# Two convolution layers on one core: every engine in the order of issue, stores a step behind, loads placed by hand

## The chip, the cores and the metric

The kernel runs on one core of a Trainium2 chip. A core has TensorE (PE, matrix multiply, with its weight loads shown as PEld), VectorE (DVE), ScalarE (ACT), GpSimd (POOL) and SyncE (SP). SP issues all of this kernel's data transfers; they run on 16 DMA engines. The metric is the device time of one execution in microseconds (us), as a median of runs. The profile is of one further execution.

## The reference

The input x is 4 x 512 x 64 x 64 in float32. Layer 0 is a linear attention with a convolved second set of heads; layer 1 takes edge maps of the result, mixes channels and normalizes.

```python
# layer 0
qkv = concat(h @ wq.T, h @ wk.T, h @ wv.T)             # channels last, then moved back
dw  = conv(qkv, dw_kernel, 5x5, groups=1536)
pw  = conv(dw, pw_kernel, 1x1, groups=192)
f   = concat(qkv, pw).reshape(B, -1, 24, N)            # 128 heads of 8
query, key, value = relu(f[:, :, :8]), relu(f[:, :, 8:16]), f[:, :, 16:]
scores = einsum('bhdn,bhen->bhde', pad_ones(value), key)
out = einsum('bhde,bhen->bhdn', scores, query)
out = out[:, :, :-1] / (out[:, :, -1:] + 1e-15)
y = batchnorm(conv(out, proj_kernel, 1x1)) + x
# layer 1, on y
sobel = sqrt(sobel_h**2 + sobel_v**2 + 1e-8); lap = abs(dwconv(y, K_LAP))
diag = max(abs(dwconv(y, K_D1)), abs(dwconv(y, K_D2)))
grad = sqrt(sobel**2 + lap**2 + 1e-8)
ef = gelu(bn(einsum('kbchw,koc->kbohw', stack(sobel, lap, diag, grad), w_branch)))
att = sigmoid(gelu(ef.mean((2, 3)) @ w_att1.T + b_att1) @ w_att2.T + b_att2)
z = einsum('bchw,oc->bohw', ef * att, w_fuse) + b_fuse
out = gelu(layernorm_over_channels(z) * ln_gamma + ln_beta) + y
```

## The kernel before

**Tiling.** Each of the 4 batches has 4 groups of 128 channels of q, k and v. An image is cut into 8 strips j of 512 positions (two halves of 4 strips; strip k of a half holds every fourth row). A 128x512 tile in float32 is the usual unit; a matrix product of that size is two passes of PE.

**The front: layer 0.** For each of the 16 groups `keys_and_values` and then `queries` list steps. In `keys_and_values` the steps are `project(KEY, j)` and `values(j)` for each strip, with transposes (`turn`) and `scores` behind them, and between these the second half of the previous group's convolution work (the list entries made by `q`). `project` (L250) multiplies a strip of x by the group's weights; ACT copies the result to `strip`, and four transfers put it into `inp`, the padded image that `convolve` reads. `values` (L273) ends in four stores to `near`, a DRAM image of the values' neighbourhoods. `convolve` (L382) is the 5x5 convolution as 160 small products in two passes, 320 matmuls and as many weight loads a call; each group has a call for KEY, half 0 and 1, in `queries`, and for QUERY, half 0 and 1, in the following `keys_and_values`. `correlate` (L432) multiplies turned keys by a `near` buffer of 1 MB; two calls use one buffer, and `load_near` (L420) fetches buffers in order into three slots. `denominators`, `invert` (an add and a reciprocal, L353 and L354), `spread_out` (the `over` matmuls) and `divide` make the quotient; `fold` and `conv_fold` make the output projection's weights, stored in `folded`. `mix` (L469) loads `projc` and multiplies it for batch 0.

**The stages behind: the rest.** For a finished batch three generators follow: `project_out` (Y, L599: sums eight `hd` tiles with `fold_sb` to y, adds x from `xr`, stores it from `yt`), `edge_branches` (E, L654: for each window of four rows two calls of `edges`, one for each half of the channels, and two of `branches`) and `fuse_out` (F, L746: attention, the last product, layer norm, output). Each `yield` gives the worth of a step; `advance` (L868) takes steps from the head of the list `behind` as the front earns due time, at a rate `pace`. What a batch has left when the front ends is done in a tail: 16 steps of the last batch's Y, then its E with one step of whatever remains (Y, then the F of batch 2) after each of its steps, then its own F.

**What sets the order.** PE runs in the order in which the program issues its instructions:

```python
    ctx.enter_context(tc.manual_schedule(engines={mybir.EngineType.PE}))
```

The order on ACT, DVE, POOL and on SP's queue is chosen at compile time by a scheduler that moves an instruction ahead of others when it expects it to be ready. On each engine, once so ordered, an instruction that waits holds all those behind it. A tile's buffer is free when its last reader is done; a load into it waits for that.

Of the kernel before, what the change touches and what calls it, by code (L numbers as in the profile page):

```python
# [65 lines left out]

WAIT_Y, WAIT_E, WAIT_F = 20.0, 12.0, 16.0
# [13 lines left out]
def conv_seq_kernel(  # L81
# [16 lines left out]
    ctx.enter_context(tc.manual_schedule(engines={mybir.EngineType.PE}))  # L98
# [72 lines left out]

    def load_constants():
        nc.sync.dma_start(out=consts_sb, in_=consts)
        nc.sync.dma_start(out=vec_sb, in_=vec)
        nc.sync.dma_start(out=batt1_sb, in_=batt1)

        nc.scalar.activation(inv0, vec_sb[:, V_BNV, :], AF.Sqrt, bias=bn0_eps)
        nc.vector.reciprocal(inv0, inv0)
# [3 lines left out]

        gamma_row = work_tile("gamma_row")
        nc.sync.dma_start(out=inv0_row, in_=bn0[1])
        nc.sync.dma_start(out=gamma_row, in_=bn0[0])
        nc.scalar.activation(inv0_row, inv0_row, AF.Sqrt, bias=bn0_eps)
# [25 lines left out]

    xs = {}

    class Group:
# [15 lines left out]
        def load_mat(self, t):  # L231

            dp = gw.tile([P, 4, 48], F32, name="dp_sb", tag="dp_sb", bufs=2)
            nc.sync.dma_start(out=dp, in_=dpk[self.g, t // QUERY])
            self.mat[t] = gw.tile([P, 4, 40, 8], F32, name="mat", tag="mat")
# [7 lines left out]
        def load_x(self, j):  # L243
            xs[self.b, j] = []
            for n in range(2):
                xt = xst.tile([P, 2, 512], F32, name="xt")
                nc.sync.dma_start(out=xt, in_=x[self.b, j, :, 2 * n : 2 * n + 2, :])
                xs[self.b, j] += [xt[:, 0, :], xt[:, 1, :]]

        def project(self, t, j):  # L250
            half, k = STRIPS[j]
            if (self.b, j) not in xs:
                self.load_x(j)
# [5 lines left out]
            if t == QUERY and not (j in KV_ORDER[:2] and self.g < NG - 1):  # L259
                del xs[self.b, j]  # L260
# [4 lines left out]
            for n in range(4):  # L265
                nc.sync.dma_start(out=inps[t][r::4, n, b : b + 8, :], in_=rows(s)[32 * n : 32 * n + 32, :, :])
# [6 lines left out]
        def values(self, j):  # L273
# [8 lines left out]
            if j not in Q_ORDER[:2]:  # L282
                del xs[self.b, j]
# [5 lines left out]
            for a in range(2):  # L289
                for jp in range(2):  # L290
                    nc.sync.dma_start(
                        out=self.near_dram[jp, b + a : b + a + 7 : 2, 2 : W + 2, (k + 2) % 4, :].rearrange(
                            "c x d -> x c d"
                        ),
                        in_=vt[64 * a : 64 * a + 64, :, 2 * jp : 2 * jp + 2, :].rearrange("p c q d -> p c (q d)"),
                    )
# [36 lines left out]
        def fold_turn(self):  # L333
# [4 lines left out]
            nc.scalar.copy(self.st, t_ps[:, 0:P])  # L338
            self.p = work_tile("p")
            nc.sync.dma_start(out=self.p, in_=proj[self.g])  # L340

        def fold(self):
# [4 lines left out]
            nc.sync.dma_start(out=self.folded[0, :, self.g, :], in_=f)  # L347
# [24 lines left out]
        def divide(self, half):  # L372
            banks = self.spread_out(self.rec)
            for k in range(4):
# [3 lines left out]
                nc.sync.dma_start(out=self.heads[j, :, self.g, :], in_=q)  # L378
# [53 lines left out]
        def correlate(self, half, jp, step):  # L432
# [17 lines left out]
            if step % 2:  # L450
                del self.near[half, jp, b]
                self.load_near(1)
# [16 lines left out]
        def mix(self):  # L469

            self.pc = work_tile("pc")
            if self.b:
                nc.sync.dma_start(out=self.pc, in_=mixed[self.g])
                return
            rest = work_tile("projc")
            nc.sync.dma_start(out=rest, in_=projc[self.g])
            pw = mini.tile([P, 8], F32, name="pw")
            nc.sync.dma_start(out=pw, in_=pwk[self.g])
            pwb = mini.tile([P, 16, 8], F32, name="pwb", bufs=1)
            nc.vector.tensor_mul(  # L480
                pwb, bdmask.rearrange("p (h d) -> p h d", d=8), pw.unsqueeze(1).to_broadcast([P, 16, 8])
            )
            ps = ps_tile("mix")
            nc.tensor.matmul(ps, lhsT=pwb.rearrange("p h d -> p (h d)"), rhs=rest, start=True, stop=True)
            nc.scalar.copy(self.pc, ps)
            nc.sync.dma_start(out=mixed[self.g], in_=self.pc)
# [32 lines left out]
        def conv_fold(self):  # L519
# [5 lines left out]
            nc.sync.dma_start(out=self.folded[1, :, self.g, :], in_=f)  # L525
# [502 lines left out]
```

## Time and profile before

| | us |
|---|---|
| median of 3 runs | 5160.07 (5154.5 to 5172.19) |
| the profiled execution | 5156.95 |
| its span, first to last instruction | 5155.2 |
| SP, time spent in issuing transfers | 1953 |

| engine | busy us | share of the span |
|---|---|---|
| PE | 4721.2 | 92% |
| PEld (overlaps PE) | 2727.4 | 53% |
| DVE | 2125.2 | 41% |
| ACT | 1622.7 | 31% |
| POOL | 384.0 | 7% |

An engine's busy time doesn't count its waits. A row of waits names the engine and line that stood idle, what ended the wait, the total, the number of times and the longest. "issue" means that the wait ended with nothing that the profile shows. A row of a timeline gives start, duration, engine, line, operation and tiles, and in brackets the idle time before it. TensorE's clock is given as a share of full speed. 910 MB went over the DMA engines in the span, 177 GB/s on average.

### The profile page before, as it was taken

The page shows a single profiled execution, that of the slowest core. Times are in us where ns is not written, and L with a number is a line of the kernel's source. Part 1 is how long each engine was busy: PE and PEld are TensorE (multiplying, and loading weights), DVE is VectorE, ACT ScalarE, POOL GpSimd, SP SyncE. Part 2 cuts the span into 40 slices and gives each one's busy share as a digit, 9 for nine tenths or more (in the row PEclk, how much of TensorE's full clock was granted, in tenths as well). Part 3 has the DMA queues.
Part 4 walks back from the last instruction along what each step waited for, and adds up shares of the span by engine and source line. Part 5 has one row for each costly group of instructions (what it writes and reads, how often), then busy time and mean ns, then how long its engine had stood idle before and what let it go on. Part 6 is the DMA issues. An engine that isn't in the chain of part 4 may idle for free. (4 is left out here: it accounts for less than half of the span.)

```text
span 5155.2 us, 107053 instructions
## 1 busy us (share of the span) xinstructions
PE 4721.2 (92%) x46362; PEld 2727.4 (53%) x46362; DVE 2125.2 (41%) x2960; ACT 1622.7 (31%) x2585; POOL 384.0 (7%) x291
## 2 busy tenths in 40 slices
PE   7899999998999999799999998989989998899877
PEld 4556555454566655344466655444446565345443
DVE  1222221113655625211456543431135556246975
ACT  1111111001444524200235442430024445125765
POOL 0000000000000003200000000320000000000225
PEclk9999999999999999899999999999999999899989
DMA  6777777775666666767667666567666665674535
GB/s 184 187 193 195 185 212 191 179 160 140 194 184 193 194 191 188 212 153 150 168 178 208 170 191 186 180 202 172 154 177 173 178 183 160 176 179 117 153 103 169
DMA packets 645992, 910.30 MB, mean 177 GB/s; under 512 B 323688, under 2 KB 394376, under 8 KB 627088
## 3 DMA queue, kind: packets, MB, share of 16 engines
q1 hardware_dynamic: 645520, 903.45, 65.5%
q8 instruction: 364, 5.96, 0.5%
q14 instruction: 108, 0.88, 0.1%
HBM read 622.13 MB, written 213.98 MB: 162 GB/s over the span
## 5 line engine op out<-in xcount | busy, mean ns | idle before, releaser
L256 PE MATMUL proj<-xt,w_sb 128*128 128x512 f32 x2048 | 959.6, 611 | 58.3 <-DMA xt<-in_x 47.2
L642 PE MATMUL yps<-hd,fold_sb 128*128 128x512 f32 x2048 | 904.3, 598 | 25.2 <-DMA hd<-heads 23.1
L390 PE MATMUL cv<-inp,mat 32*32 32x512 f32 x20480 | 771.7, 621 | 121.2 <-issue 112.0
L256 PEld LDWEIGHTS proj<-xt,w_sb 128*128 128x128 f32 x2048 | 382.8, 195 | 534.8 <-issue 457.1
L642 PEld LDWEIGHTS yps<-hd,fold_sb 128*128 128x128 f32 x2048 | 385.8, 191 | 510.5 <-issue 474.2
L390 PEld LDWEIGHTS cv<-inp,mat 32*32 32x32 f32 x20480 | 422.1, 105 | 433.5 <-issue 270.8
L717 PE MATMUL br<-maps,wbr_sb 128*128 128x256 f32 x2048 | 491.6, 393 | 56.6 <-ACT maps L700 33.7
L278 PEld LDWEIGHTS val<-w_sb,xt 128*128 128x128 f32 x4096 | 471.5, 192 | 31.6 <-issue 21.9
L717 PEld LDWEIGHTS br<-maps,wbr_sb 128*128 128x128 f32 x2048 | 395.6, 196 | 173.5 <-issue 55.8
L278 PE MATMUL val<-w_sb,xt 128*128 128x128 f32 x4096 | 484.1, 276 | 0.1
L795 PE MATMUL zps<-ef,wf_sb 128*128 128x512 f32 x1024 | 462.6, 604 | 21.0 <-DVE z L799 7.2
L262 ACT COPY strip<-proj 128x512 f32<-128x512 f32 x256 | 149.3, 583 | 1017.1 <-PE proj L256 952.8
L647 DVE SCALAR_TENSOR_TENSOR yt<-yps,shift,xr 128x512 f32<-128x512 f32 x128 | 96.1, 751 | 905.1 <-PE yps L642 833.7
L442 PE MATMUL corr<-near,ckt 128*32 128x160 f32 x8192 | 330.7, 313 | 28.1 <-DMA near<-near 23.0
L236 POOL TENSOR_TENSOR mat<-dp_sb 128x1280 f32<-128x1280 f32 x32 | 77.3, 2416 | 3484.1 <-PE cv L390 2959.3
L795 PEld LDWEIGHTS zps<-ef,wf_sb 128*128 128x128 f32 x1024 | 194.2, 193 | 263.8 <-issue 227.8
L442 PEld LDWEIGHTS corr<-near,ckt 128*32 128x32 f32 x8192 | 252.4, 110 | 130.0 <-issue 58.2
L690 DVE TENSOR_TENSOR maps<-dv 128x1054 f32<-128x1054 f32 x128 | 162.6, 1270 | 304.1 <-PE br L717 304.1
L724 ACT ACTIVATE ef_o<-br,shift,scale 128x256 f32<-128x256 f32 x256 | 142.4, 560 | 314.9 <-PE br L717 314.4
L306 ACT ACTIVATE kt<-tr 128x512 f32<-128x512 f32 x128 | 76.1, 595 | 496.5 <-PE tr L304 488.9
L354 DVE RECIPROCAL rec<-rec 128x512 f32<-128x512 f32 x64 | 214.5, 3351 | 1.4
L402 ACT ACTIVATE co<-cv 128x512 f32<-128x512 f32 x128 | 74.6, 597 | 438.5 <-PE cv L390 438.4
(124 smaller groups left out, 4096.6 us busy)
## 6 DMA issues: line engine op xcount, KB each, us to landing
xt<-in_x SPq DMA_DIRECT2D x400, 512.0 KB
near<-near SPq DMA_DIRECT2D x128, 1056.0 KB
inp<-strip SPq DMA_DIRECT2D x1024, 64.0 KB
win<-y SPq DMA_DIRECT2D x128, 396.0 KB
near<-vt SPq DMA_DIRECT2D x512, 66.0 KB
y<-yt SPq DMA_DIRECT2D x128, 264.0 KB
yr<-y SPq DMA_DIRECT2D x128, 264.0 KB
xr<-in_x SPq DMA_DIRECT2D x128, 256.0 KB
```

The source lines that it names most:

```text
L256: nc.tensor.matmul(ps, lhsT=self.w[t][:, c, :], rhs=xs[self.b, j][c], start=(c == 0), stop=(c == NCH - 1))
L262: nc.scalar.copy(s, ps)
L278: nc.tensor.matmul(ps[:, ts(c, P)], lhsT=xs[self.b, j][n][:, ts(c, P)], rhs=self.w[VALUE][:, n, :], start=(n == 0), stop=(n == NCH - 1),)
L354: nc.vector.reciprocal(rec, rec)
L390: nc.tensor.matmul(rows(banks[i])[32 * j : 32 * j + 32, :, c0:c1], lhsT=self.mat[t][q, j, (dx + 2) * 8 + 4 * b : (dx + 2) * 8 + 4 * b + 4, :],
L442: nc.tensor.matmul(self.banks[jj][32 * i : 32 * i + 32, 160 * b : 160 * b + 160], lhsT=self.held["c", i][:, at : at + 32], rhs=v[:, 4 * n ...
L642: nc.tensor.matmul(ps, lhsT=fold_sb[g // NG][:, g % NG, ts(c, P)], rhs=hd[g], start=(g == 0), stop=(g == 2 * NG - 1),)
L647: nc.vector.scalar_tensor_tensor(yt[:, :, 1 : W + 1], rows(ps), shift0[:, c : c + 1], rows(xr), ALU.add, ALU.add)
L690: nc.vector.tensor_sub(flat[:, half : 3 * half - 2], dvs[:, 2 : 2 * half], dvs[:, 0 : 2 * half - 2])
L717: nc.tensor.matmul(rows(ps)[:, 4 * n : 4 * n + 4, :], lhsT=wbr_sb[:, k, c, :], rhs=rows(maps[c // 2][:, slot[k], c % 2, :], WB)[:, :, 0:W] ...
L724: nc.scalar.activation(o[:, n, :], ps[:, 256 * n : 256 * n + 256], AF.Gelu, bias=shift1[:, k : k + 1], scale=scale1[:, k : k + 1], accum_o ...
L795: nc.tensor.matmul(ps, lhsT=wf_sb[:, k, ts(c, P)], rhs=ef[k], start=(k == 0), stop=(k == 3))
```

## The change

The whole program becomes manual: all engines and SP run in the order of issue. A list `waiting` holds closures with a step number; `later` appends, `tick`, called after every step, issues those whose step has come. `send` is a store put off in this way by a step, and all stores but the zero borders go through it.

- Loads of x follow a fixed list `x_order`, half a strip each. Five are issued at the start; `done_x` asks for two more a step after a strip's last use. Before, `project` loaded a strip that wasn't there.
- `load_near`, `load_w`, `load_mat`, `load_p`, `load_pc` and `load_wtab` become entries of worth 0 in the lists of steps; `correlate` no longer loads. `make_mat` on POOL comes three steps after its load. The constants' arithmetic comes three steps after their loads, the zero borders of `near` at steps 6 and 14.
- Y loads `fold_sb` in eight pieces, each followed by an `hd` tile, a step each; `xr` is loaded one step ahead, with 2 buffers for 3; `yt` has 3 buffers for 2.
- E is cut by half windows p (channel half and four rows) into `load_window`, `columns`, `across`, `laplacian`, `gradient` and `roots`; the gradient and roots of p-1 come with the `across` of p, the branches of a window a step later still. The operations are the same. With the last batch a flush of all waiting stores stands before each window load.
- F loads `ef` with 7 buffers for 8 (three tiles of the next strip after the first product, the rest after the last). `norm` becomes `variance`, a reciprocal a step later and `finish` for one or two channel tiles at a time, over two strips' steps; `z` has 8 buffers for 6, `sq` 2 for 3.
- The tail issues 22 steps of the F of batch 2 beside the first 24 of Y (8 of them its loads), and then spreads the rest over E in proportion to `FILL_Y` and `FILL_F`.

```diff
+FILL_Y, FILL_F = 1.5, 3.5
+REST = 16 * FILL_Y + 11 * FILL_F
...
-    ctx.enter_context(tc.manual_schedule(engines={mybir.EngineType.PE}))
+    ctx.enter_context(tc.manual_schedule())
+    waiting, clock = [], [0]
+    def later(issue, steps=1):
+        waiting.append((clock[0] + steps, issue))
+    def tick(whole=False):
+        clock[0] += 1
+        ready = [w for w in waiting if whole or w[0] <= clock[0]]
+        waiting[:] = [w for w in waiting if not (whole or w[0] <= clock[0])]
+        for _, issue in ready:
+            issue()
+        if whole and waiting:
+            tick(True)
+    def send(out, in_, steps=1):
+        later(lambda: nc.sync.dma_start(out=out, in_=in_), steps)
...
+    def done_x(b, j):
+        del xs[b, j]
+        later(lambda: load_x(2))
...
             if step % 2:
                 del self.near[half, jp, b]
-                self.load_near(1)
...
         def queries(self):
...
-                pj(0), own("scores", KV_ORDER[6]), own("turn", KV_ORDER[7]), pj(1), cv(0), pj(2), own("scores", KV_ORDER[7]), ct(0, 0), ct(0, 1), pj(3),
-                ct(0, 2), ct(0, 3), own("denominators", 1), own("fold_turn"), pj(4), own("divide", 1), pj(5), co(0, 0),
-                own("fold"), pj(6), co(0, 2), co(1, 0), co(1, 2), cv(1), pj(7), ct(1, 0), ct(1, 1), own("denominators", 0),
-                ct(1, 2), ct(1, 3),
+                pj(0), own("scores", KV_ORDER[6]), own("turn", KV_ORDER[7]), ld("load_mat", QUERY), pj(1), cv(0), pj(2),
+                ld("load_w", KEY, of=after), own("scores", KV_ORDER[7]), ct(0, 0), ct(0, 1), pj(3), near, ct(0, 2), ct(0, 3),
+                own("denominators", 1), ld("load_p"), own("fold_turn"), near, pj(4), own("divide", 1), near,
+                ld("load_w", VALUE, of=after), pj(5), co(0, 0), near, co(0, 2), own("fold"), pj(6), co(1, 0), co(1, 2), cv(1),
+                pj(7), ct(1, 0), ct(1, 1), near, own("denominators", 0), ct(1, 2), ct(1, 3),
...
         def keys_and_values(self, before):
...
+                pj(KEY, 0), near(before), q("conv_sums"), ld("load_mat", KEY), pj(VALUE, 0), near(before), q("divide", 0),
+                ld("load_w", QUERY), pj(KEY, 1), pj(VALUE, 1), co(0, 0), tr(0), near(before), pj(KEY, 2), co(0, 2),
+                pj(VALUE, 2), sc(0), tr(1), co(1, 0), pj(KEY, 3), co(1, 2), ld("load_wtab"), ld("load_pc", of=before),
...
     def project_out(b, heads, cheads, folded, side):
...
+            for g in range(2 * NG):
+                nc.sync.dma_start(out=fold_sb[g // NG][:, g % NG, :], in_=folded[g // NG, :, g % NG, :])
+                load(0, g + 1)
+                yield WAIT_Y / (2 * NG)
...
     def edge_branches(b, efs, pool_sb, side):
...
+            load_window(0)
+            yield WAIT_E
+            for p in range(4 * NJ + 2):
+                ready = p // 2 - 1 if p >= 2 and p % 2 == 0 else None
+                if p < 4 * NJ:
+                    columns(p)
+                    load_window(p + 1)
+                    yield 3.0 * share
+                if 1 <= p <= 4 * NJ:
+                    gradient(p - 1)
+                if p < 4 * NJ:
+                    across(p)
+                if 1 <= p <= 4 * NJ:
+                    roots(p - 1)
+                    yield 4.5 * share
+                if ready is not None:
+                    branches(ready, (1, 2))
+                    yield 1.5 * share
+                if p < 4 * NJ:
+                    laplacian(p)
+                    yield 5.0 * share
+                if ready is not None:
+                    branches(ready, (0, 3))
+                    del maps[2 * ready], maps[2 * ready + 1]
+                    yield 1.5 * share
+            tick(True)
...
     next(fused)
     next(edged)
-    for _ in range(1 + NCH * NJ // 2):
-        next(projected)
-    rest = [projected] + behind
-    for n, _ in enumerate(edged):
-        while rest and next(rest[0], None) is None:
-            rest.pop(0)
+    for n in range(6 + NCH * NJ // 2):
+        next(behind[0])
+        tick()
+        for _ in range(1 if n >= 6 else 2 if n >= 2 else 0):
+            next(projected)
+            tick()
+    rest, spent, given = [projected] + behind, 0.0, 0.0
+    for share in edged:
+        tick()
+        given += share * REST / SHARE_E
+        while rest and spent < given:
+            step = next(rest[0], None)
+            if step is None:
+                rest.pop(0)
+            else:
+                spent += FILL_Y if rest[0] is projected else FILL_F
+                tick()
```

## The prediction

> **What bounds the kernel now.** I read the page first, then TensorE's waits, then the places that the long waits point to.
>
> ```profile
> span 5155.2 us, 107053 instructions
> PE 4721.2 (92%) x46362; PEld 2727.4 (53%) x46362; DVE 2125.2 (41%) x2960; ACT 1622.7 (31%) x2585; POOL 384.0 (7%) x291
> core 0: 5155.2 us, clock 0.963
> ```
>
> TensorE (PE) is the bound: busy for 4721 us, idle for 434. The second loss is in the clock. A window that isn't at 1.00 is at 0.50, so a mean of 0.963 is 0.037 x 2 x 5155 = 381 us at half rate, of which PE was busy for about 251 by the trace's clock records: some 126 us of slowness on top of the idle time. The change leaves the arithmetic as it is, so all that it can win is in these 434 + 126 = 560 us. TensorE's waits by what ended them:
>
> ```profile
> PE cv L390 <- issue: 112.0, 46, 4.4
> PE proj L256 <- DMA xt<-in_x: 47.2, 14, 12.1
> PE br L717 <- ACT maps L700: 33.7, 9, 10.2
> PE over L369 <- DVE rec L354: 23.6, 16, 4.6
> PE yps L642 <- DMA hd<-heads: 23.1, 6, 9.8
> PE corr L442 <- DMA near<-near: 23.0, 7, 19.6
> PE heads_ps L511 <- ACT strip L262: 20.4, 1, 20.4
> PE mix L484 <- DMA projc<-in_projc: 14.2, 4, 4.9
> ```
>
> The first row counts most: in `convolve` PE waited 112 us for nothing that the profile names. I cut the convolve matmuls into their 64 calls. The second KEY half takes 19.0 us on average, the first KEY half 11.4, the two QUERY halves 12.3 and 13.0, an undisturbed call 10.6. Of the 121 us of such idle time inside the calls, 78 lie in that one call of each group. Windows over an undisturbed call (first row) and three of the slow ones; columns are window, length, busy time of PE, PEld, DVE, ACT and POOL, clock, share of the DMA engines, GB/s:
>
> ```profile
> 679.00:689.60 10.60, 10.60 (x321) 6.54 (x320) 0.00 (x0) 1.09 (x2) 0.00 (x0) 1.00 0.70 226
> 161.00:181.00 20.00, 13.70 (x321) 6.81 (x317) 1.82 (x4) 0.59 (x2) 0.00 (x0) 0.91 0.84 210
> 352.00:369.00 17.00, 13.22 (x324) 7.35 (x321) 2.10 (x4) 0.39 (x1) 0.16 (x1) 0.90 0.98 247
> 2600.00:2618.00 18.00, 14.75 (x324) 7.82 (x320) 2.06 (x4) 0.00 (x0) 0.00 (x0) 0.81 0.83 194
> ```
>
> The timeline of SyncE (SP), then of PE, around the last of these says why:
>
> ```profile
> 2590.23 0.57 SPq L427 DMA_DIRECT2D near<-near  x1
> ...
> 2594.02 1.22 SPq L427 DMA_DIRECT2D near<-near  x2
> ...
> 2600.19 0.52 SPq L427 DMA_DIRECT2D near<-near  x1
> ...
> 2600.05 7.13 PE L390 MATMUL cv<-inp,mat 32*32 32x512 f32 x182
> 2610.44 7.92 PE L390 MATMUL cv<-inp,mat 32*32 32x504 f32 x138 [3.25 <-issue]
> ```
>
> Four `near` loads of 1 MB are issued in the 10 us up to this call's start. A convolve call issues 640 instructions in 10.6 us[...]. The page's queue list has an instruction queue, q8, with 364 packets of 16 KB[...]. In the trace a q8 packet starts about 2.6 us before most of these waits end, and the DMA engines were nearly full for the 6 us before it. I read the row as instruction blocks stuck behind bulk loads.
>
> **The change part by part.** A minus is time saved.
>
> (A) `near` loads. Before, every second `correlate` fetches the next buffer, so three or four of these megabytes land just before or in `convolve(KEY, 1)`. After, three are issued from `project(3)` to `divide`, the fourth after the first `correlate` pair, the fifth only after that call and the last projection. The call should come down to a QUERY call's 12.5: 16 x (19.0 - 12.5) = -104. The fourth now flows under the second correlate pair, which is as dense (128 instructions in 2.45 us): a third of a 3.3 us stall each, +19. Sum -85. Ends: 0 if density alone makes the stall, -134 if the call reaches 10.6. [...]
>
> (B) `mix`: projc is loaded right where it is used; after, `load_pc` issues it some five steps and one 10.6 us call ahead. -14.2, and half a 3.4 us half-rate window after each of four: -6.8. Sum -20.
>
> (C) Start: at 26.5 us PE waits 12.1 for the second strip of x, since SP stood at a store of `vt` with the x loads behind it. After, two and a half strips are issued first. -13 with the clock.
>
> (D) heads_ps, 20.4 at 1247: ACT held four relus of a convolve that ended at 1217 behind three half-windows of edge work. In order of issue the relus come first. With the clock -22.
>
> (E) `near` at 2165, 19.6: the load waited on SP behind eight `hd` and two `fold_sb` transfers. After, the four-step lead covers most; the 16 transfers still share the engines. -15.
>
> (F) x loads elsewhere: 47.2 - 5.6 (first load, stays) - 12.1 (C) = 29.5. After, a load follows the release of its buffer by one step, 1.5 strips ahead. -25. (G) `hd`: fold_sb in eight pieces, each beside its `hd`: half of 25, -12.
>
> (H) over <- rec, 23.6 in 16: at 1334 DVE put an edge step of 1.25 us between the add and the 3.35 us reciprocal. In order they are adjacent; another 6.4 of this wait is a weight-mean reduction that stood ahead of a reciprocal. With the clock -20.
>
> (I) The tail, after 4430:
>
> ```profile
> 4430.00:4560.00 130.00, 119.45 (x275) 52.30 (x272) 18.88 (x26) 1.20 (x4) 0.22 (x4) 0.94 0.80 200
> 4560.00:4700.00 140.00, 138.92 (x384) 72.34 (x383) 78.43 (x116) 56.28 (x74) 0.00 (x0) 1.00 0.69 164
> 4700.00:5000.00 300.00, 231.08 (x692) 139.04 (x690) 278.66 (x328) 235.19 (x322) 82.35 (x56) 0.89 0.43 131
> 5000.00:5155.00 155.00, 122.76 (x278) 52.38 (x277) 81.99 (x77) 72.04 (x90) 73.06 (x56) 0.91 0.47 147
> ```
>
> VectorE (DVE) bounds 4700 to 5000: 279 of 300 us busy, and PE waits 69. After, 22 steps of batch 2's fusion (18 of them 3.6 us of PE, plus the variance matmuls, some 68) go beside the first 16 projection steps (7.15 each, 114), where DVE is free; 16 projection and some 14 fusion steps are spread over the edges. First part 182 + 10 to fill. Edges: a window of four rows costs DVE 17.0 us (eleven operations from 0.71 to 1.27, twice) and PE 7.3 (two branch pairs). With 2.7 projection steps each the first six are PE's, about 27 us; with 1.4 fusion steps each the other ten are DVE's, about 21: 372. Then 154 as now. 182 + 10 + 372 + 154 = 718 against 725. I take -10 for fewer half-rate windows; ends -45 (edges at DVE's 20 throughout) and +40 (25 a window: a `yt` on DVE waits 7 us for its matmuls with the edges queued behind it).
>
> Sum: 85 + 20 + 13 + 22 + 15 + 25 + 12 + 20 + 10 = 222.
>
> (J) The price: ACT, DVE, POOL and SP now wait in program order. After a convolve PE stands in front of this ACT queue: four relus 2.4, a root with its table load 2.45, two gelus with theirs 2.8, two squares and an absolute value 2.8 = 10.4 us before the next strip copy. PE's cover is four PSUM tiles: a branch pair 3.7, a projection 3.6, scores 0.5, two transposes 1.0 = 8.8. It runs dry by 1.6 us. The nearest row agrees: proj <- ACT ckt L417 waited 9.2 us in 5 times. There are 33 convolves beside edge work; at 1.9 idle and 1.1 of half rate (two in three), 33 x 3.0 = +100. Below: 0, if the cover holds. Above: 10 us each, +330.
> [...] But a wait of 1.89 us ending at 1339.2 was followed by this:
>
> ```profile
> 1339.90:1343.30 3.40, 3.40 (x8) 1.25 (x5) 3.04 (x6) 2.61 (x3) 0.00 (x0) 0.50 0.42 131
> ```
>
> So short waits cost it too; I keep 100.
>
> SP's stores come a step later and its loads queue behind stores that wait for that step's engines. SP issued for 1953 us of the span and the loads placed by hand have two or more steps (7 us and up) of lead, so I price this at nothing; a lead that fails shows as PE waiting on a DMA. The 24 extra `fold_sb` issues cost SP 24 x 0.54 = 13 us, inside its waiting. The additional memsets are 0.11 us each on POOL, 7% busy.
>
> 5155.2 - 222 + 100 = 5033. The profiled run was 1.75 us longer than its span and 3.1 below the median shown, so 5038; I round to 5035.
>
> **The rivals.** (R1) Density, not `near`, makes the fetch wait: A is 0, 5120. For it: the slow calls follow six dense correlate steps. Against: the first KEY half, with the DMA engines 0.64 busy on average, hardly stalls. (R2) ACT's order costs nothing and the tail gains 45: 5035 - 100 - 35 = 4900. For it: ACT is 31% busy. (R3) Slower. DVE's `across` waits for PE's last branch matmuls (the page has 304.1 us of idle before L690, 2.4 for each of 128). In order of issue every evacuation, reciprocal and `yt` behind it waits too, and PE runs out of PSUM tiles. If PE loses that 2.4 and half the time 1.7 of clock in each of the 96 half-windows ahead of the tail, 96 x 3.25 = 312 in place of (J): 5245. It decides from 222/96 = 2.3 us a half-window. Against: the page's DVE is busy for only 41%. (R4) What waits won is paid back in others, within 0.3%.
>
> **How the numbers follow.** Forecast 0.50 (4960 to 5100), R1 0.10, R2 0.12, R3 0.23, R4 0.05. The runs spread by 0.3%, which is about what can be told from no change. Faster 0.5 + 0.1 + 0.12 = 0.72, same 0.05, slower 0.23. Range 4900 to 5200: R2's end below, a mild R3 above.
>
> **What would show it.** The second KEY convolve near 12.5 us; `mix`, heads_ps and xt gone from the waits; clock above 0.97; new rows of PE waiting for an ACT strip or ckt. Wrong if those rows or PE on DVE sum to over 220 us, or if issue stays at 112.

## The result: 7.3% slower, because loads now arrive late

The changed kernel takes 5538.57 us (median), against 5159.53 for the kernel before: a ratio of 1.0731, 95% interval 1.0711 to 1.0752. I had forecast 5035. The profile after has these lines at the head of its page, and these waits of TensorE (us in total, times, longest):

```profile
span 5534.0 us, 107036 instructions
PE 4827.5 (87%) x46362; PEld 2778.4 (50%) x46362; DVE 2152.2 (39%) x2960; ACT 1579.6 (29%) x2567; POOL 361.6 (7%) x299
core 0: 5534.0 us, clock 0.942
```

```profile
PE corr L480 <- DMA near<-near: 196.5, 52, 10.9
PE yps L701 <- DMA hd<-heads: 89.8, 27, 6.9
PE zps L907 <- DMA ef<-ef: 70.6, 15, 9.0
PE br L805 <- DVE dv L759: 45.5, 6, 10.5
PE cv L428 <- issue: 44.1, 37, 3.9
PE br L805 <- ACT maps L789: 36.2, 8, 7.0
PE den L398 <- ACT rq L307: 30.9, 24, 5.0
...
PE over L407 <- DVE rec L392: 13.8, 13, 6.5
PE proj L294 <- ACT ckt L455: 13.5, 4, 8.6
PE proj L294 <- DMA xt<-in_x: 13.3, 3, 5.6
```

Three rows of before have grown: `near` from 23.0 to 196.5, `hd<-heads` from 23.1 to 89.8, `ef` from 2.6 to 70.6. The row of `ef` in before was:

```profile
PE zps L795 <- DMA ef<-ef: 2.6, 1, 2.6
```

The sum of the three is 357 of 687.5 us of idle time. They grew by 308 us together, and all idle time by 277. `cv <- issue` fell from 112.0 to 44.1, and the row of `mix` is gone. The arithmetic is the same: 46362 matmuls in both. PE's busy time rose by 106 us; 94 of them are the longer time at half rate.

One sum serves for the rest of the document. From the traces I add PE's waits over 150 ns (idle) and the time that PE was busy while the clock records show half rate (half). The records of before and after hold 1.00 and 0.50 and nothing between: 62 stretches at 0.50 in before, 387 us in all, and 102 in after, 643 us. Span less idle less half of half is 4619 us in before, 4627 in after, and between 4611 and 4636 in every profile below. So little else moves the time: a span is some 4625, within 15, plus idle plus half/2. From before to after, idle went from 410.5 to 687.5 and half from 251 to 438: 277 + 94 = 371 of the 379 us between the spans.

What a late load looks like: the timeline of SyncE (SP) and then of PE at the third strip of a `project_out`. Columns are start, length, engine, line, operation, tiles, count, and the idle time before it.

```profile
1005.54 0.33 SPq L688 DMA_DIRECT2D xr<-in_x  x1
...
1011.05 0.38 SPq L120 DMA_DIRECT2D y<-yt  x1
1011.52 0.71 SPq L677 DMA_DIRECT2D hd<-heads  x1
1012.32 2.92 SPq L679 DMA_DIRECT2D hd<-cheads  x4
```

```profile
1008.08 2.54 PE L480 MATMUL corr<-near,ckt 128*32 128x160 f32 x64
1010.55 1.12 PE L382 MATMUL fold<-p,stt 128*128 128x512 f32 x2
1011.51 2.74 PE L701 MATMUL yps<-hd,fold_sb 128*128 128x512 f32 x6
1018.64 6.26 PE L701 MATMUL yps<-hd,fold_sb 128*128 128x512 f32 x10 [4.39 <-DMA hd<-heads]
```

Three of the eight `hd` tiles of the next strip are loaded early; the other five wait for buffers. In after they are issued by `later`, one step on, and behind the `y<-yt` store of the strip's last product, which waits on DVE. The store went out at 1011.05, the fourth tile at 1011.52, and PE was through the first three tiles at 1014.25. The tile released PE at 1018.64, 7.1 us after its issue. The load was not slow; it was asked for when PE was at the door.

The trace shows what held SP before that. Up to 1005.52 it stood for the landing of a `near` load issued at 992.68. Then it issued an `xr` load at 1005.54, which landed at 1010.08; DVE, which needs it for `yt`, began at 1010.27, and the store followed. So one late transfer made the next late. Here `xr` held `yt` up; in 115 of the 125 waits before a `yt` in after DVE waited for PE's product.

`near` shows the same. Lead from the issue of a load to the moment PE needs it (median over the 16 groups), by the eight buffers of a group in order, worked out from the two traces:

| buffer | 1 | 2 | 3 | 4 | 5 | 6 | 7 | 8 |
|---|---|---|---|---|---|---|---|---|
| before: lead, us | 127 | 90 | 91 | 9 | 56 | 60 | 67 | 17 |
| before: PE waited, us in all | 0 | 0 | 0 | 22 | 0 | 0 | 0 | 1 |
| after: lead, us | 8.2 | 11.4 | 6.8 | 5.2 | 25 | 20 | 20 | 12.8 |
| after: PE waited, us in all | 28.5 | 43.5 | 28.2 | 66.5 | 0 | 0 | 0 | 29.8 |

A megabyte that is asked for beside the other traffic took 7.7 to 16.3 us from its issue to the release of PE, 10.1 in the median, over the 52 times that PE waited for one. The first two of group 1, in the same two views (SP, then PE):

```profile
316.09 0.59 SPq L465 DMA_DIRECT2D near<-near  x1
316.73 0.59 SPq L378 DMA_DIRECT2D p<-in_proj  x1
317.36 0.56 SPq L465 DMA_DIRECT2D near<-near  x1
```

```profile
319.92 3.70 PE L294 MATMUL proj<-xt,w_sb 128*128 128x512 f32 x8
325.46 2.55 PE L480 MATMUL corr<-near,ckt 128*32 128x160 f32 x64 [1.84 <-DMA near<-near]
331.42 2.54 PE L480 MATMUL corr<-near,ckt 128*32 128x160 f32 x64 [3.41 <-DMA near<-near]
```

The first was issued at 316.09 and released PE at 325.46, the second at 317.36 and at 331.42.

### The profile page after: what moved, and what is told of

Same layout as the page of the kernel before. It is cut to its first block, busy times and chain, and to the rows that moved or that the text cites. A ratio compares the mean times of both kernels' runs of the same rounds, so it can differ in the third digit from the quotient of the medians.

```text
span 5534.0 us, 107036 instructions
## 1 busy us (share of the span) xinstructions
PE 4827.5 (87%) x46362; PEld 2778.4 (50%) x46362; DVE 2152.2 (39%) x2960; ACT 1579.6 (29%) x2567; POOL 361.6 (7%) x299
## 5 line engine op out<-in xcount | busy, mean ns | idle before, releaser
L701 PE MATMUL yps<-hd,fold_sb 128*128 128x512 f32 x2048 | 953.8, 618 | 114.1 <-DMA hd<-heads 89.8
L294 PE MATMUL proj<-xt,w_sb 128*128 128x512 f32 x2048 | 953.7, 609 | 31.2 <-ACT ckt L455 13.5
L428 PE MATMUL cv<-inp,mat 32*32 32x512 f32 (+1 forms) x20480 | 739.4, 596 | 45.7 <-issue 44.1
L805 PE MATMUL br<-maps,wbr_sb 128*128 128x256 f32 x2048 | 505.7, 402 | 107.3 <-DVE dv L759 45.5
L480 PE MATMUL corr<-near,ckt 128*32 128x160 f32 x8192 | 380.4, 344 | 202.1 <-DMA near<-near 196.5
L907 PE MATMUL zps<-ef,wf_sb 128*128 128x512 f32 x1024 | 477.5, 614 | 73.2 <-DMA ef<-ef 70.6
L480 PEld LDWEIGHTS corr<-near,ckt 128*32 128x32 f32 x8192 | 281.1, 122 | 321.8 <-DMA near<-near 156.9
L913 DVE TENSOR_SCALAR z<-zps,fbias 128x512 f32<-128x512 f32 x128 | 94.7, 740 | 495.0 <-ACT sq L911 196.6
L497 DVE TENSOR_TENSOR weighed<-corr,wtab_sb 128x320 f32<-128x320 f32 x128 | 62.1, 486 | 502.6 <-PE corr L480 483.2
```

Source lines behind the costliest of these rows:

```text
L294: nc.tensor.matmul(ps, lhsT=self.w[t][:, c, :], rhs=xs[self.b, j][c], start=(c == 0), stop=(c == NCH - 1))
L428: nc.tensor.matmul(rows(banks[i])[32 * j : 32 * j + 32, :, c0:c1], lhsT=self.mat[t][q, j, (dx + 2) * 8 + 4 * b : (dx + 2) * 8 + 4 * b + 4, :],
L480: nc.tensor.matmul(self.banks[jj][32 * i : 32 * i + 32, 160 * b : 160 * b + 160], lhsT=self.held["c", i][:, at : at + 32], rhs=v[:, 4 * n ...
L701: nc.tensor.matmul(ps, lhsT=fold_sb[g // NG][:, g % NG, ts(c, P)], rhs=hds[j][g], start=(g == 0), stop=(g == 2 * NG - 1),)
L805: nc.tensor.matmul(rows(ps)[:, 4 * n : 4 * n + 4, :], lhsT=wbr_sb[:, k, c, :], rhs=rows(maps[2 * u + c // 2][:, slot[k], c % 2, :], WB)[:, ...
L907: nc.tensor.matmul(ps, lhsT=wf_sb[:, k, ts(c, P)], rhs=efts[j][k], start=(k == 0), stop=(k == 3))
```

## The experiments

Two theories stood against each other. **L**: SP's queue in program order issues loads late; the compute engines' order matters little. **C**: the in-order compute engines (step J, rival R3) carry most of the loss. All runs are variants of the changed kernel unless said otherwise. The manual schedule lists the engines that run in program order; the others are placed by the scheduler. The kernel before has TensorE alone in the list. A ratio is to runs of before made alongside, with its 95% interval in the text; idle and half are those of the profiled execution.

| run | in program order | loads and tail | median us | ratio to before | idle / half, us |
|---|---|---|---|---|---|
| before | PE | before | 5159.53 | | 410 / 251 |
| after | all | after | 5538.57 | 1.0731 | 687 / 438 |
| sp_free | all but SP | after | 5215.8 | 1.0112 | 448 / 305 |
| sp_order | PE, SP | after | 5441.0 | 1.0550 | 627 / 413 |
| near_early | all | three `near` moved up | 5475.13 | 1.0614 | 626 / 448 |
| hd_ef_direct | all | `hd`, `ef` ahead of the store | 5340.32 | 1.0356 | 550 / 344 |
| spaced | all | those, and `near` spread out | 5150.58 | 0.9982 | 406 / 245 |
| spaced_tail | all | spaced, tail's order as before | 5200.75 | 1.0074 | 448 / 232 |
| sp_free_tail | all but SP | tail's order as before | 5246.72 | 1.0171 | 479 / 290 |
| no_order | none | after | 5084.28 | 0.9852 | 343 / 214 |
| pe_only | PE | after | 5120.93 | 0.9927 | 389 / 228 |
| before_free | none | kernel before | 5145.36 | 0.9971 | 380 / 272 |
| s_pe | PE, SP | spaced | 5123.05 | 0.9926 | 394 / 235 |
| s_pe_act | PE, SP, ACT | spaced | 5097.82 | 0.9889 | 387 / 230 |
| s_pe_dve | PE, SP, DVE | spaced | 5122.39 | 0.9933 | 377 / 224 |
| s_sp | SP | spaced | 5057.92 | 0.9803 | 322 / 200 |

**sp_free and sp_order: which queue's order costs?**

```diff
-    ctx.enter_context(tc.manual_schedule())
+    ctx.enter_context(tc.manual_schedule(engines={mybir.EngineType.PE, mybir.EngineType.Activation, mybir.EngineType.DVE, mybir.EngineType.Pool}))
```

> Same program, but SyncE's queue is left to the scheduler; TensorE, ScalarE, VectorE and GpSimd keep the order of issue. Theory L (late loads: the order on SyncE's queue starts near, hd and ef too late): TensorE's waits for these three fall from 381 us together to some 50, as before the change, and the time to about 5150. Theory C (the order on the compute engines costs, the late loads are only its symptom): waits of TensorE stay near 690 us in sum, time over 5450.

> The other half: SyncE and TensorE in the order of issue, ScalarE, VectorE and GpSimd left to the scheduler. Theory L: near, hd and ef waits stay near 380 us, time 5480 to 5560. Theory C: the time falls to about 5200.

sp_free took 5215.8 (ratio 1.0112, 1.0087 to 1.0136), sp_order, with the list {PE, SP}, 5441.0 (1.0550, 1.0517 to 1.0583). Freeing SP alone takes off 323 us; freeing ACT, DVE and POOL instead takes off 98. Three waits of TensorE in sp_free:

```profile
PE cv L428 <- issue: 114.3, 55, 4.8
...
PE corr L480 <- DMA near<-near: 30.3, 9, 5.9
...
PE yps L701 <- DMA hd<-heads: 12.6, 5, 8.7
```

The late loads are gone, and the idle time inside the convolves is back: the scheduler issues `near` early again (the first buffer 123 us ahead of its use in the median, 127 in before, 8.2 in after), and the second KEY convolve takes 17.7 us again (11.9 in after, 19.0 in before). So SP's order did two things: it brought that stall down and made the loads late. L was right on the place; sp_free stayed 66 us above the 5150 that L gave, so C's share is not nothing.

**near_early: are the `near` loads late, and what do they hit if they come earlier?** The first three loads of a group move to the end of the key phase.

```diff
                 pj(VALUE, 6), pj(KEY, 7), q("conv_divide", 1), sc(5), tr(6), pj(VALUE, 7),
+                near(self), near(self), near(self),
...
-                ld("load_w", KEY, of=after), own("scores", KV_ORDER[7]), ct(0, 0), ct(0, 1), pj(3), near, ct(0, 2), ct(0, 3),
-                own("denominators", 1), ld("load_p"), own("fold_turn"), near, pj(4), own("divide", 1), near,
+                ld("load_w", KEY, of=after), own("scores", KV_ORDER[7]), ct(0, 0), ct(0, 1), pj(3), ct(0, 2), ct(0, 3),
+                own("denominators", 1), ld("load_p"), own("fold_turn"), pj(4), own("divide", 1),
```

> All engines in the order of issue; the three near loads that stand in the queries at the third projection, the fold and the divide are moved to the end of the keys and values, some 60 us ahead of their use; the fourth and the four others stay. Theory L: the waits of the first three (28 + 44 + 28 = 100 us) go, with a third of that again in half-rate clock: about 5400. The fourth's 66 us stay if its lead of 5 us is the cause, and fall if the first three in flight were. Theory C: within 1% of 5538. Second KEY convolve stays near 12 us, since nothing lands in it.

5475.13 (1.0614, 1.0591 to 1.0638), 63 us below after, where about 138 were expected. TensorE's waits:

```profile
PE cv L428 <- issue: 89.2, 42, 4.8
...
PE corr L480 <- DMA near<-near: 66.7, 17, 6.9
```

`near` lost 130 us of wait, as it should; the three moved loads never make PE wait, and the fourth's wait fell from 66.5 to 36.5. But `issue` doubled, and the convolve cut shows where: the first KEY call rose from 12.2 to 16.4 us, the second stayed at 11.9. The two timelines (SP, then PE) of one group:

```profile
281.62 3.04 SPq L465 DMA_DIRECT2D near<-near  x3
```

```profile
285.94 8.02 PE L428 MATMUL cv<-inp,mat 32*32 32x512 f32 x236
297.35 5.77 PE L428 MATMUL cv<-inp,mat 32*32 32x504 f32 x84 [3.40 <-issue]
```

Three megabytes issued in the 4 us ahead of a dense call, and PE stands for 3.40 us inside that call. The stall moved with the loads, while the calls' own instructions stayed, so R1 (density alone) falls. That PE waits for instructions there is a reading of the queue that the page calls instruction, q8, with 364 packets of 16 KB, in number one for every 255 of PE's 92724 matmuls and weight loads: all 28 of these waits over 1 us ended 1.3 to 2.3 us after the end of a q8 packet, 1.5 in the median, and the 40 of before did the same (1.2 to 2.2). In the 6 us ahead of those 40 packets the 16 DMA engines were full in most cases (a busy share of 1.0 in the median, 0.56 at the least). No record says what a q8 packet holds, so step (A)'s reading, instruction blocks stuck behind bulk loads, fits all of this and isn't proved by it. The second KEY call, with no `near` load just ahead of it, stayed at 11.9 us.

**hd_ef_direct: load ahead of the store.** The rest of the next strip is loaded in the step of the last product, ahead of that step's `yt` store.

```diff
-                    send(y[c, :, at : at + 29 : 4, :], yt)
                     if c == 0:
                         load(j + 1, deep - 2 * NG)
                     if c == NCH - 1:
                         del hds[j]
-                        later(lambda j=j: load(j + 1, 2 * NG))
+                        load(j + 1, 2 * NG)
+                    send(y[c, :, at : at + 29 : 4, :], yt)
...
-                    later(lambda: load(j + 1, 4))
+                    load(j + 1, 4)
```

> All engines in the order of issue; in the output projection and the fusion the loads of the next strip's hd and ef tiles are issued in the step of the last product, ahead of that step's store, and no longer at the tick after it. Theory L: hd and ef waits (114 + 71 us) fall below 60 and the time to about 5390. Rival: the tiles come free only as the last product reads them, so the store ahead cost nothing: waits over 140 us, time over 5480.

5340.32 (1.0356, 1.0335 to 1.0377): 198 us for three lines, 50 more than expected. Waits:

```profile
PE yps L701 <- DMA hd<-cheads: 24.3, 13, 5.6
...
PE zps L907 <- DMA ef<-ef: 6.3, 1, 6.3
PE yps L701 <- DMA hd<-heads: 6.3, 5, 3.4
```

Lead is what changed: for the fourth `hd` tile of a strip the median went from 5.5 us back to 9.5 (10.7 in before), for the fourth `ef` from 4.1 to 5.0. The median hides the gain for `ef`: in after 12 of the 32 loads were issued when PE already stood waiting, here one. That step took `yps <- hd<-heads` from 89.8 to 6.3. Idle fell by 137 and half by 94, so 137 + 47 of the 195.5 us between the spans; about a quarter of the gain is clock.

**spaced: all loads early, none just ahead of a KEY convolve.** hd_ef_direct, and the `near` loads spread out; the first correlate pair moves up by one projection in both phases to free its buffer sooner.

```diff
-                ld("load_w", QUERY), pj(KEY, 1), pj(VALUE, 1), co(0, 0), tr(0), near(before), pj(KEY, 2), co(0, 2),
+                ld("load_w", QUERY), pj(KEY, 1), co(0, 0), near(before), pj(VALUE, 1), tr(0), pj(KEY, 2), co(0, 2),
...
-                pj(VALUE, 6), pj(KEY, 7), q("conv_divide", 1), sc(5), tr(6), pj(VALUE, 7),
+                pj(VALUE, 6), pj(KEY, 7), q("conv_divide", 1), sc(5), tr(6), near(self), pj(VALUE, 7),
...
-                pj(0), own("scores", KV_ORDER[6]), own("turn", KV_ORDER[7]), ld("load_mat", QUERY), pj(1), cv(0), pj(2),
+                pj(0), own("scores", KV_ORDER[6]), own("turn", KV_ORDER[7]), ld("load_mat", QUERY), pj(1), cv(0), near, pj(2),
...
-                own("denominators", 1), ld("load_p"), own("fold_turn"), near, pj(4), own("divide", 1), near,
-                ld("load_w", VALUE, of=after), pj(5), co(0, 0), near, co(0, 2), own("fold"), pj(6), co(1, 0), co(1, 2), cv(1),
+                own("denominators", 1), ld("load_p"), own("fold_turn"), pj(4), own("divide", 1), co(0, 0), near,
+                ld("load_w", VALUE, of=after), pj(5), co(0, 2), own("fold"), pj(6), co(1, 0), co(1, 2), cv(1),
```

> All engines stay in the order of issue. hd and ef as in hd_ef_direct; the near loads are spread out with three steps or more of lead, none in the steps just before a KEY convolve: the first in the last key step, the second after the first KEY convolve, the first correlate pair moved one projection up so that the fourth load has some 12 us. Late loads (L): TensorE's wait for near falls from 196 to under 50 us, the issue rows of both KEY convolves stay small (under 20 us each), the half-rate time falls with the waits: 5130 to 5190. If the megabytes only trade places with the instruction fetch (near_early did that), the near wait falls and the issue row grows past 90 again: 5250 or more.

5150.58 (0.9982, 0.9972 to 0.9992): 388 us below after, with every engine still in the order of issue. TensorE's waits:

```profile
PE cv L428 <- issue: 54.9, 41, 3.5
PE br L805 <- DVE dv L759: 44.5, 6, 10.3
PE br L805 <- ACT maps L789: 38.5, 8, 6.5
PE den L398 <- ACT rq L307: 31.2, 24, 4.8
...
PE corr L480 <- DVE q L415: 23.1, 15, 4.2
...
PE corr L480 <- DMA near<-near: 13.5, 5, 7.8
```

The leads of the eight `near` loads are now 44, 28, 22, 13, 20, 20, 20 and 17 us, and six of the eight never make PE wait. Both KEY convolves keep near 12 us (12.6 and 12.0). So the place of the loads is the whole loss against before; SP may stay in order if the loads have their lead. Two runs from below say it once more: with TensorE and SP in order, s_pe and its spaced loads (5123.05) are level with pe_only, where SP is free (5120.93); sp_order, with the loads of after, is 320 above it (5441.0).

**spaced_tail and sp_free_tail: is the new tail the rest?** The tail in the program order of before: projections alone, then one step of the rest after another among the edges.

```diff
-FILL_Y, FILL_F = 1.5, 3.5
-REST = 16 * FILL_Y + 11 * FILL_F
+FILL_Y, FILL_F = 1.0, 1.0
+REST = 16 * FILL_Y + 37 * FILL_F
...
-    for n in range(6 + NCH * NJ // 2):
-        next(behind[0])
+    for n in range(2 * NG + NCH * NJ // 2):
+        next(projected)
         tick()
-        for _ in range(1 if n >= 6 else 2 if n >= 2 else 0):
-            next(projected)
-            tick()
```

> The loads of spaced, and the tail in the program order of before: sixteen projection steps of the last batch alone, then fusion and projection steps one by one among the edge steps. If the new tail cost what the windows show (837 us against 725), most of it through work put side by side, this is 60 to 110 us below spaced: 5040 to 5120. If the tail is longer because its engines run in order, whatever the program, it stays within 25 us of spaced.

> The queue of SP left to the scheduler as in sp_free (5216), and the tail in the program order of before. If the tail's new program is what sp_free still lost: 5120 to 5160, with TensorE's wait for edge maps down from 111 to about 50 us. If the compute engines' order costs it: 5190 to 5220, with those rows as they were.

Both went the other way: 5200.75 (1.0074, 1.0049 to 1.0099) is 50 us above spaced, 5246.72 (1.0171, 1.0142 to 1.0201) 31 above sp_free. The tail, from the last `over` matmul to the end, takes 795 us in spaced_tail against 750 in spaced; `br <- ACT maps L789` rose from 38.5 to 84.6, but `br <- DVE dv` fell from 44.5 to 8.9. What grew in sum are the tail's waits for `hd` (1.3 to 27.3, `heads` and `cheads` together) and for `ef` (1.6 to 18.2). I had taken the longer tail of after (825 us against 723.5) for a fault of its program. It is not.

**no_order, pe_only and before_free: what is the program worth without the order?**

```diff
-    ctx.enter_context(tc.manual_schedule())
...
+    ctx.enter_context(tc.manual_schedule(engines={mybir.EngineType.PE}))
```

The first line alone is no_order, with the second it is pe_only; before_free is the kernel before without its own such line.

> The program of after with no engine in the order of issue (the scheduler orders all five as it did before). If the order of the compute engines is what sp_free lost (61 us), this is 5140 to 5170. If it is the new program (the tail, finer steps, loads put elsewhere), it stays at 5200 or more.

> The program of after with the mode of the kernel before: TensorE alone in the order of issue (no_order freed it too, which before did not). If TensorE's order costs 65 us here as between s_sp and s_pe: 5130 to 5165, the new program is worth nothing by itself, and in-order ACT, DVE and POOL cost 50 to 85 on top (sp_free is 5216). If the program is what gained in no_order: 5080 to 5105, and step (J), priced at 100, was 110 to 135.

> The kernel before with TensorE left to the scheduler as well, nothing else changed. If freeing TensorE is worth some 65 us in any of these programs: 5080 to 5110. If it needs the changed program's smaller steps: 5145 or more.

The text for no_order has an error of mine: the kernel before did hold TensorE in order, so that run freed one engine more than it says. no_order took 5084.28 (0.9852, 0.9827 to 0.9877), pe_only 5120.93 (0.9927, 0.9894 to 0.9960), before_free 5145.36 (0.9971, 0.9961 to 0.9981). So the changed program in the mode of before is 39 us faster than before; the expected values, 5130 to 5165 or 5080 to 5105, lie on either side of that. Freeing TensorE is worth 37 us in the changed program, 15 in the old one.

By the profiles, the 39 us are all in the tail. The last `over` of the front ends at 4435.8 us in pe_only and at 4431.6 in before; the tail takes 683 against 723.5. The windows of the tail of after, then of pe_only, cut at the first edge operation and at the last branch matmul (columns: window, length, busy time of PE, PEld, DVE, ACT, POOL, clock, share of the DMA engines, GB/s):

```profile
4709.00:4942.00 233.00, 214.13 (x476) 91.98 (x476) 54.23 (x64) 41.82 (x52) 38.85 (x38) 0.96 0.66 179
4942.00:5344.00 402.00, 283.59 (x822) 175.90 (x820) 302.56 (x399) 232.50 (x324) 31.35 (x24) 0.85 0.41 108
5344.00:5534.00 190.00, 136.00 (x290) 58.28 (x288) 73.36 (x78) 74.14 (x95) 68.18 (x56) 0.86 0.44 136
```

```profile
4436.00:4617.00 181.00, 180.69 (x417) 79.63 (x418) 58.80 (x62) 40.77 (x50) 40.05 (x33) 0.99 0.76 192
4617.00:4976.00 359.00, 290.28 (x880) 176.22 (x878) 294.49 (x401) 241.01 (x332) 54.80 (x25) 0.92 0.53 136
4976.00:5119.00 143.00, 121.59 (x288) 54.62 (x288) 78.50 (x78) 73.69 (x95) 71.89 (x56) 0.93 0.54 164
```

By the waits of PE inside these windows, the first stretch of after lost 17 us to `hd`, the last 30 to `ef`, and `hd` took another 12 in the edges. The edges themselves lost 105 us to `br` waiting for maps, against 65 in pe_only: DVE is busy for 303 of 402 us there, for 294 of 359 in pe_only, and the clock is 0.85 against 0.92.

**s_sp, s_pe, s_pe_act, s_pe_dve: which engine's order costs, once the loads are on time?** The program of spaced, with one engine after another in the list; for s_pe_dve:

```diff
-    ctx.enter_context(tc.manual_schedule())
+    ctx.enter_context(tc.manual_schedule(engines={mybir.EngineType.PE, mybir.EngineType.DVE, mybir.EngineType.SP}))
```

> The program of spaced; only SP stays in the order of issue, the compute engines and POOL are the scheduler's. If compute order costs some 130 us whatever SP does (sp_free against no_order): 5020 to 5060, and the second KEY convolve stays at 12 us. If SP's order is only good beside engines that run in the same order: stores and loads stand behind work that the scheduler has moved back, and it is 5120 or more.

> The program of spaced; SP and TensorE in the order of issue, ACT, DVE and POOL the scheduler's. If TensorE's own order costs nothing: within 10 us of s_sp. If it is what costs: near spaced, 5130 to 5150.

> The program of spaced; SP, TensorE and ACT in the order of issue, DVE and POOL the scheduler's. By step (J), relus and copies behind edge work on ACT: 5120 to 5150. If DVE's order is the cost: within 25 us of s_pe.

> The program of spaced; SP, TensorE and DVE in the order of issue, ACT and POOL the scheduler's. By rival R3 (DVE's queue in order): 5110 to 5150, with the waits of edge maps on dv (44 us) and of correlate on q (23 us) as in spaced. By (J): within 25 us of s_pe, with these rows gone.

s_sp took 5057.92 (0.9803, 0.9777 to 0.9828), the fastest of all, 102 us below before. s_pe (0.9926, 0.9904 to 0.9949) is 65 above it, s_pe_act (0.9889, 0.9862 to 0.9915) 25 below s_pe, s_pe_dve (0.9933, 0.9911 to 0.9955) level with s_pe, spaced 28 above s_pe. So TensorE's own order is the dearest here, ACT's seems to help (the two intervals still touch), and neither ACT nor DVE alone makes the 100 of step (J). POOL's order was not tried alone. Waits of TensorE in s_sp, then in s_pe:

```profile
PE br L805 <- ACT maps L789: 41.4, 13, 15.2
...
PE corr L480 <- DVE q L415: 25.9, 11, 4.7
...
PE over L407 <- DVE rec L392: 10.5, 3, 4.3
```

```profile
PE br L805 <- ACT maps L789: 78.8, 14, 13.3
PE corr L480 <- DVE q L415: 54.2, 16, 7.7
...
PE over L407 <- DVE rec L392: 34.2, 18, 7.4
```

A free TensorE has other matmuls where it would wait for DVE: in s_sp other tiles' matmuls (320 of them correlates, 61 us of busy time in all) stand inside the convolve calls, none do in s_pe, and PE's waits on DVE fall from 94.5 to 41.3 us. The gain is in the front, which ends at 4346.5 us in s_sp and at 4412.4 in s_pe.

"Level" hides two things in s_pe_dve: with DVE in order the front ends 41 us earlier than in s_pe (4370.9), and the tail takes 30 more (744 against 714). With ACT in order the front ends 22 us earlier and the tail takes 9 more. Why each of the two helps the front, and why little of it is left when all are in order (spaced: 4406.2 and 750), stays open.

## Why the prediction was wrong

Fixing the engines one after another in the changed program gives the whole of it: before 5160, pe_only 5121 (program, -39), sp_free 5216 (ACT, DVE and POOL in order, +95), after 5538 (SP in order, +323). By the other way, over sp_order, SP costs 320 and the other three 98. The prediction had -222 for its gains, +100 and 0. The first of these doesn't match the -39 exactly, since (A) and (D) need engines in order.

**The step that failed** is the last of the change part by part: "SP's stores come a step later and its loads queue behind stores that wait for that step's engines", and yet "the loads placed by hand have two or more steps (7 us and up) of lead, so I price this at nothing". It measured +323. Two errors are in it. A lead of 7 us was set against no landing time; `near` took 7.7 to 16.3. And lead was counted in steps of the list; the last `hd` and `ef` of a strip had one step, with a store ahead of them, and SP itself stood for 586 us in 102 waits for a `yt`. Moving these loads alone took off 198, moving `near` as well 190 more. The sentence named its own test (a lead that fails shows as PE waiting on a DMA), and that is what the waits show.

**The second miss** is smaller. Of the 503 us between forecast and result 388 went with the loads. The other 115 lie in the sum of gains: with the loads mended and ACT, DVE and POOL free (s_pe) it came to 37 us instead of 222, while (J), from there to spaced, took 28 instead of 100. The gains were priced as if no new wait would come; the last part of this section tells which ones came.

**(A)** named the right loads: the second KEY convolve came to 11.9 us (forecast 12.5), the `issue` row to 44.1. The 19 us set aside there (16 times a third of 3.3 makes 17.6) were for fetches that the fourth `near` would hold up; what came was a wait for that load itself, 66.5, and for others that were to have 7 us and more of lead. And it is the order on SP that brings the gain: with SP free it is gone (the second KEY convolve takes 17.3 us in pe_only, 11.3 in sp_order).

**(B)**, **(C) and (F)** came nearly as said: the row of `mix` is gone, xt went from 47.2 to 13.3 (some 10 were to stay). **(D)** too, 20.4 to 1.0, but only in order: in pe_only one wait of 23.0 on `co` and one of 17.6 take its place. **(E)** and **(G)** turned round, part of the failed step. **(H)**: 23.6 fell to 13.8 and the weight mean's 6.4 went, but `csb` appeared with 6.4: 10 us of waiting instead of 20 with the clock.

**(I)**: the three stretches were put at 192, 372 and 154; pe_only has 181, 359 and 143. So there the tail was worth -40, near the end of -45 that I gave; but this is with TensorE alone in order, which the prediction was not about. In order it takes 750 us with the loads mended (+26), and with the late loads of after 825 (+102).

**(J)** had the size by luck, and not the place. In-order ACT, DVE and POOL cost 95 beside a free SP, but 28 in spaced, all of it in the tail (750 us against 714 in s_pe); `proj <- ckt` rose from 9.2 to 13.5 only, so the 33 convolves aren't it. R3 falls as well: it looked for its loss ahead of the tail, and there s_pe_dve is 41 us faster than s_pe.

**What waits won was paid back.** With the loads mended, spaced has 406 us of idle where before has 410. Sorted by what ended them, PE's waits on DMA fell from 120 to 73 us and on `issue` from 118 to 57; its waits on ACT rose from 96 to 126, on DVE from 71 to 134 and on POOL from 4 to 16.5. So 108 us were won and 106 paid back, above all in `den <- rq` (8.9 to 31.2), `corr <- q` (3.5 to 23.1) and `br <- dv` (new, 44.5). Two rows of before, for comparison with those of spaced:

```profile
PE den L360 <- ACT rq L269: 8.9, 18, 1.0
...
PE corr L442 <- DVE q L377: 3.5, 2, 2.4
```

In time, the front won 25 us (it ends at 4406.2 against 4431.6) and the tail gave 26 back. That is R4, but for spaced and not for the kernel that was forecast. R2's two halves came in different runs: ACT's order cost nothing in s_pe_act, and the tail gained 40 in pe_only.

For each microsecond of a short wait, step (J) charged 0.58 us of time lost at half rate: a half-rate stretch after two waits in three, an estimate for which it showed one wait of 1.89 us. The clock records say less often. Of PE's waits of 1.5 to 2 us in before, 7 of 23 have a half-rate stretch that starts between the wait's start and 3.5 us after its end; in after 5 of 27. Of the 97 shorter ones of before (over 150 ns) it is 2, of the 20 of 2 to 3 us 14, of the 45 longer ones 43. From s_sp to after idle grew by 366 us and half by 239, of which half is lost: 0.33 for each microsecond, over waits of all lengths. No run here prices short waits alone.

## What to carry to other kernels

When a queue goes from the scheduler to program order, the place of a load in the program becomes its time of issue: for each load, take its measured time from issue to landing under load (here 7.7 to 16.3 us for a `near` load that PE waited for), and count back from its use in microseconds, with the stores and other transfers that the queue must get through first. Look at what a bulk load stands in front of, too: here the same megabytes cost a wait when they came late (196.5 us for `near` in after), a stall inside the convolve when they came just ahead of it (89.2 us of `cv <- issue` in near_early), and less of both together when spread out (13.5 and 54.9 us in spaced). Put in order only the queue that gains by it: here SP alone, with the loads placed by lead, was 2.0% faster than before (1.7 to 2.2) and the fastest of all.

## What the runs showed of the hardware

- The stall inside the convolves follows the bulk loads: the second KEY call took 19.0 us in before and 11.9 in after, and the first went from 12.2 to 16.4 when three `near` loads were put 4 us ahead of it (near_early).
- In these runs waiting came with a lower clock, which added about a third to its cost (from s_sp to after 366 us more of idle and 239 us more at half rate, half of which is lost).
- SP's transfers held each other up. In the traces of before, after and spaced they signal their landing on eight semaphores in rotation, and before a transfer is issued SP waits for the landing of the one eight places earlier, which has the same semaphore (3592 of the 3697 such transfers of after wait for it right before they are issued). In after SP stood so for 602 us in 498 waits, half of it (299 us) for `near`; in before for 181 us in 179. All 60 stores of the row below wait for the semaphore that they are to signal themselves; they do not read that tile. In spaced it is 526 us, without a loss against before, so these waits alone didn't cost PE here; more semaphores weren't tried.

```profile
SPq L120 <- DMA near<-near: 198.2, 60, 5.3
```
